# New costs for the planner of an attention, pairwise-tanh and recurrence kernel

## The chip, the cores and the metric

The kernel runs on one core of a Trainium2 chip, in fp32. The metric is the device time of one launch in microseconds (us). The core has five engines that each run their own queue of instructions in order: TensorE (PE; its weight loads are PEld), VectorE (DVE), ScalarE (ACT), GpSimd (POOL) and SyncE (SP, which issues transfers). An instruction that needs the result of another engine waits for a semaphore, and all that stands behind it in its queue waits with it.

## The reference

Eight batches of 1024 tokens of 128 channels go through two layers. Layer 0 is attention with 8 heads and two softmaxes, a feed-forward net and two layer norms. Layer 1 has an attention whose scores are sums of a tanh over all pairs of tokens, and then a recurrence over the 1024 tokens with a batch norm before it. Cut to what matters:

```python
# layer 0
scores = einsum('bhlfc,bhmgc->bhlfmg', q, k) / sqrt(c)     # 1024 x 1024 for each of 8 heads
a = softmax(softmax(scores, axis=4), axis=5)
z = einsum('bhlfmg,bhmgc->bhlfc', a, v)
z1 = layer_norm(z @ wo.T + bo + x)
x = layer_norm(relu(z1 @ w1.T + b1) @ w2.T + b2 + z1)
# layer 1, attention: t is x as tokens, B = norm(t)
Wi = einsum('bnd,ed->bne', B, W)
s = einsum('d,bijd->bij', v, tanh(Wi[:, None, :, :] + Wi[:, :, None, :]))
t = t + einsum('bij,bjd->bid', softmax(s), B)
# layer 1, recurrence: y_t = sigmoid(batch_norm(W norm(t))_t + y_{t-1} V^T), added to t
```

The pairwise tanh is the largest part: 1024 x 1024 / 2 pairs by 128 channels in each batch (the scores are symmetric, so half is computed).

## The kernel before

**Work and tiles.** `layer0(b)` walks over 8 heads and, for each head, over 8 blocks of 128 queries. A block is a chain across engines: scores on PE (L851, into one of two buffers `sc`), the first exponential on ACT (L854), sums over one axis and their reciprocal on DVE (L858, L859), the division on DVE (L862, into a pair buffer `e` in `wx`). For two blocks together follow the second exponential on ACT (L871), sums and reciprocal on DVE (L874, L875), two divisions on POOL (L885), sixteen transposes on PE (L765), four copies of banks on DVE (L777), sixteen matmuls "attend" on PE (L899) and a sum into `zs` on DVE (L906). There are 256 such pairs in all.

`layer1(b)` computes the pairwise tanh. For each block of 128 rows it builds groups of k rows: a row of `wiT` plus one column as bias, by ACT at once with the tanh (L993, one instruction a row), or added by POOL (L1000) or DVE (L996 or L1000) with one whole-group tanh on ACT behind it (L1036). The group lies in one of five slots `th`. PE then multiplies each row with `v` (L1053), four row groups side by side in a narrow tiling mode, into `sa`. When a block of rows is complete, ACT takes the exponential of `sa` (L1149), and attention, projection and statistics follow.

After the last batch there are the recurrence and the output (from L1321 on), written in plain program order.

**What sets the order.** All of this is not emitted as the loops run. Each piece is an entry in a `Plan` (class at L409): a weight in us, an engine or a choice of engines, what it reads and writes, a priority. `Plan.emit` (L455) then runs a list schedule in its own notion of time. For each entry it knows when it is ready: the planned end of what it depends on, plus `LATENCY` of the engine that made it, or `AGAIN` if that is the same engine. It takes the engine with the earliest possible start, looks at all entries there that can start within 0.15 us (`slack`) of it, and emits that with the lowest priority number; a change of mode on PE costs 0.1 in the plan (`switch`). The engine that builds the rows of a group is chosen the same way, by the earliest start. The planned times are used for nothing else: what reaches the chip is one order for each engine, and the waits that the dependencies need. Two PSUM banks `m0` and `m1` are shared by nearly all that goes through a bank (`through_bank`, L755); the plan also picks which of them is taken, by which was planned free first.

**Priorities** (`pace`, and `ROWS` and `L1` in `layer1`) are set so that layer 0 of batch b + 1 and layer 1 of batch b lie side by side over the whole middle of the run. Layer 0 of batch 0 stands alone at the start, and layer 1 of batch 7 at the end.

Of the kernel before, what the change touches and what calls it, by code (L numbers as in the profile page):

```python
# [15 lines left out]
P = 128  # L16
# [392 lines left out]
class Plan:  # L409
# [12 lines left out]

    LATENCY = {"PE": 0.28, "ACT": 0.2, "DVE": 0.15, "POOL": 0.3, "SP": 8.0}
    AGAIN = {"PE": 0.0, "ACT": 0.0, "DVE": 0.08, "POOL": 0.15, "SP": 8.0}

    def __init__(self):
        self.ops = []
# [131 lines left out]
def fast_path(ctx: ExitStack, tc: tile.TileContext, a: dict, fits):  # L561
# [222 lines left out]
    def layer0(b):  # L784
# [16 lines left out]
        for n_part, part in enumerate(parts):  # L801
# [3 lines left out]
            for h in range(H):  # L805
                L0 = pace(n_part, h)

                u, vp, kvp = us[h % 2], vps[h % 2], ("vp", h % 2)
                if alone:
                    vp, kvp = ths[3 + h // 4][:, h % 4 * N : (h % 4 + 1) * N].rearrange("p (t c) -> p t c", c=C), ("vp0", h)  # L810
                for s in range(2) if part is None else (part,):
                    cols = slice(s * 512, (s + 1) * 512)

                    def project(bank, h=h, cols=cols):
                        nc.tensor.matmul(bank, A[:, h, :], xT[:, cols], start=True, stop=True)

                    def biased(e, bank, h=h, u=u, cols=cols):
                        if e == "ACT":
                            nc.scalar.activation(u[:, cols], bank, AF.Identity, bias=ub[:, h : h + 1])
                        else:  # L820
                            nc.vector.tensor_scalar(u[:, cols], bank, ub[:, h : h + 1], None, ALU.add)

                    through_bank(project, 0.9, [kx], biased, evict(0.75), [], [("u", h % 2, s)], L0, banks)
                for s in () if alone and n_part else range(2):

                    def values(bank, h=h, s=s):
                        for i in range(4):
                            t = 4 * s + i
                            nc.tensor.matmul(
                                bank[:, i * P : (i + 1) * P], xT[:, t * P : (t + 1) * P], Wvo[:, h, :], start=True, stop=True  # L830
                            )

                    through_bank(
                        values, 0.95, [kx], copy(vp[:, 4 * s : 4 * s + 4, :]), evict(0.7), [], [kvp + (s,)], L0, banks
                    )
                for qt in qts:
                    L0 = pace(n_part, h + (qt - qts[0]) / len(qts))
                    i = (n_part * H + h) * len(qts) + qt - qts[0]
                    sc, kc = scs[i % 2], ("sc", i % 2)
                    pair, q = (b * H * NT + i) // 2 % NE, qt % 2  # L840
                    e2, st = es[pair], stat_e[pair]
                    e, ke = e2[:, q, :], ("e", pair, q)
                    k1, k2 = ke + (1,), ("e", pair, 2)
                    r1, r2 = st[:, q, 0:G], st[:, :, G : G + M]
                    sc3 = sc.rearrange("p (m g) -> p m g", g=G)
                    e3 = e.rearrange("p (m g) -> p m g", g=G)

                    def scores(_, sc=sc, u=u, qt=qt):
                        for s in range(2):
                            cols = slice(s * 512, (s + 1) * 512)  # L850
                            nc.tensor.matmul(sc[:, cols], u[:, qt * P : (qt + 1) * P], xT[:, cols], start=True, stop=True)  # L851

                    add(("PE", 1.81), scores, r=[kx, ("u", h % 2, qt // 4)], w=[kc], pri=L0)
                    add(("ACT", 1.02), lambda _, sc=sc: nc.scalar.activation(sc, sc, AF.Exp, scale=SCALE),  # L854
                        r=[kc], w=[kc], pri=L0)

                    def first_sums(_, sc=sc, r1=r1):
                        nc.vector.tensor_reduce(r1, sc.rearrange("p (m g) -> p g m", g=G), AX.X, ALU.add)  # L858
                        nc.vector.reciprocal(r1, r1)  # L859

                    def divide(_, e3=e3, sc3=sc3, r1=r1):
                        nc.vector.tensor_tensor(e3, sc3, r1.unsqueeze(1).to_broadcast([P, M, G]), ALU.mult)  # L862

                    add(("DVE", 1.6), first_sums, r=[kc], w=[k1], pri=L0)
                    add(("DVE", 1.22), divide, r=[kc, k1], w=[ke], pri=L0)
                    if q == 0:
                        continue


                    ks = [("e", pair, q) for q in range(2)]  # L870
                    add(("ACT", 1.93), lambda _, e2=e2: nc.scalar.activation(e2, e2, AF.Exp), r=ks, w=ks, pri=L0)  # L871

                    def second_sums(_, e2=e2, r2=r2):
                        nc.vector.tensor_reduce(r2, e2.rearrange("p q (m g) -> p q m g", g=G), AX.X, ALU.add)  # L874
                        nc.vector.reciprocal(r2, r2)  # L875

                    add(("DVE", 3.3), second_sums, r=ks, w=[k2], pri=L0)
                    na = next_aT()
                    aT = aTs[na]
                    for q in range(2):  # L880
                        e, ke = e2[:, q, :], ("e", pair, q)

                        def divide_again(_, e=e, r2=r2, q=q):
                            e3 = e.rearrange("p (m g) -> p m g", g=G)
                            nc.gpsimd.tensor_tensor(e3, e3, r2[:, q, :].unsqueeze(2).to_broadcast([P, M, G]), ALU.mult)  # L885

                        add(("POOL", 1.97), divide_again, r=[ke, k2], w=[ke], pri=L0)
                        for s in range(2):
                            through_bank(
                                transposes([e[:, t * P : (t + 1) * P] for t in range(4 * s, 4 * s + 4)]), 0.52, [ke],  # L890
                                copy(aT[:, 4 * s : 4 * s + 4, q * P : (q + 1) * P]), evict(0.7), [],
                                [("aT", na, q, s)], L0, banks,
                            )
                    q0 = (qt - 1) * P
                    bank = Bank(*banks)

                    def attend(part, vp=vp, aT=aT, bank=bank):
                        for t in range(4 * part, 4 * part + 4):
                            nc.tensor.matmul(bank()[:, :256], vp[:, t, :], aT[:, t, :], start=t == 0, stop=t == NT - 1)  # L899

                    def gather(_, h=h, q0=q0, bank=bank):
                        zq = zs[:, q0 : q0 + 2 * P]
                        if h == 0:
                            nc.vector.scalar_tensor_tensor(zq, bank()[:, :256], zb, xT[:, q0 : q0 + 2 * P], ALU.add, ALU.add)
                        else:
                            nc.vector.tensor_tensor(zq, bank()[:, :256], zq, ALU.add)  # L906

                    for s in range(2):
                        add(
                            ("PE", 1.81), lambda _, attend=attend, s=s: attend(s),  # L910
                            r=[kvp + (p,) for p in range(2)] + [("aT", na, q, p) for q in range(2) for p in range(2)],
                            w=[("bank", bank)], pri=L0, take=None if s else bank, wait=[kz + (qt // 4,)],
                        )
                    add(("DVE", 0.42), gather, r=[("bank", bank), kx], w=[kz + (qt // 4,)], pri=L0, give=bank)

            L0 = b - 1 - SOON
            for qh in range(2) if part is None else (part,):
                Xg, kg = X[:, 4 * qh : 4 * qh + 4, :], kX + (qh,)
                through_bank(
                    transposes([zs[:, t * P : (t + 1) * P] for t in range(4 * qh, 4 * qh + 4)]), 0.52, [kz + (qh,)],  # L920
                    copy(Xg), evict(0.7), [], [kg], L0, banks,
                )

                def affine1(Xg=Xg):
# [3 lines left out]
                layer_norm(Xg, kg, Xg, kg, qh, L0, affine1)  # L928
                z1T, k1 = zs[:, 512 * qh : 512 * qh + 512], kz + (qh,)
                through_bank(  # L930
                    transposes([Xg[:, i, :] for i in range(4)]), 0.52, [kg], copy(z1T), evict(0.7), [], [k1], L0, banks
                )
                na = next_aT()
                hT = aTs[na].rearrange("p t q -> p (t q)").rearrange("p (f q) -> p f q", q=512)
# [35 lines left out]
    def group(it, at0, r0, k, wiT, all_wi, L1, ROWS, fillers, chain, left, both, first_half):  # L970
# [27 lines left out]
        def add_rows(eng, c):  # L998
# [6 lines left out]

        each = [(c, r) for r in range(k) for c in range(4)]
        work = {
            "ACT": [(0.19 + 0.833e-3 * (w - begin[c]), lambda c=c, r=r: tanh_row(c, r)) for c, r in each],
            "POOL": [
                (0.27 + 1.62e-3 * k * (w - begin[c]), lambda c=c: add_rows(nc.gpsimd, c)) for c in range(4)  # L1010
            ],
# [37 lines left out]
        def times_v(_):  # L1049
# [12 lines left out]
        before = ["sa"] if at0 and r0 == 0 else ["sa", "sa narrow"] if at0 else ["sa"] if r0 else []  # L1062
        after = ["sa narrow"] if at0 and r0 == 0 else [] if r0 or at0 else ["sa"]
        add(
            ("PE", k * (1.67e-3 * (w - begin[0]) + 0.03 * n)), times_v, r=[("tanh", g)] + before,
            w=[("sa", it, r0)] + after, pri=L1, mode="groups", give=slot,
        )
        return ("sa", it, r0)
# [99 lines left out]
    def attention(b, it, X, kX, B, kB, E_at, L1):  # L1168

        for j0 in range(it + 1, NT, 4):  # L1170
# [1 line left out]
            through_bank(  # L1172
                transposes([E_sb[:, E_at[it] + j - it, :] for j in js]), 0.08 + 0.12 * len(js),
                [("E", it, j) for j in js],
                copy(ET[:, j0 - 1 : j0 - 1 + len(js), :]), ("DVE", 0.15 + 0.135 * len(js)), [],
                [("ET", j) for j in js], L1,
            )

# [274 lines left out]
```

## Time and profile before

| what | value |
|---|---|
| time, median of 3 runs | 5830.94 us (5828.89 to 5839.92) |
| profiled span | 5830.7 us, 96061 instructions |
| TensorE clock granted, mean | 0.97 |
| pairwise tanh on ACT, row by row (L993) | 3180 instructions, 2318.0 us |
| pairwise tanh on ACT, group by group (L1036) | 726 instructions, 1993.6 us |
| times v on PE (L1053) | 24576 matmul records, 2113.1 us |
| scores on PE (L851) | 2048 matmul records, 983.7 us |
| first sums on DVE (L858) | 512 instructions, 1213 ns each |
| transfers, all queues | 37.71 MB, mean 6 GB/s |

In the profile, a group of instructions is named by engine and line, with what it writes and reads. An idle time is put down to whoever ended it. A matmul's end is modelled, so the busy time of PE is not the time in which it could do nothing more; the distances between starts tell more. Successive ACT instructions overlap by a few tens of ns, so the sum over groups is a little over the busy time of the engine.

### The profile page before, as it was taken

What the parts mean: (1) busy time and instruction counts of PE and PEld (TensorE: products, weight loads), DVE (VectorE), ACT (ScalarE), POOL (GpSimd) and SP (SyncE); (2) the same over time, 40 slices, a digit from 0 to 9 for tenths busy, and PEclk for the clock granted to TensorE, in tenths of its full rate; (3) what the DMA queues carried; (4) which work ended last, traced back from release to release, by engine and by line L of the source; (5) the groups of instructions that cost most, each with busy time, mean ns of one, the idle gap of its engine ahead of it and who ended that gap; (6) DMA issues with size and microseconds to landing.
All of it is one profiled execution on the core that took longest, in us unless ns stands there. A gap on an engine that the chain in (4) does not pass through costs nothing.

```text
span 5830.7 us, 96061 instructions
## 1 busy us (share of the span) xinstructions
PE 5221.5 (90%) x38885; PEld 2786.1 (48%) x38885; DVE 4688.8 (80%) x6416; ACT 5291.4 (91%) x5032; POOL 3850.9 (66%) x2414
## 2 busy tenths in 40 slices
PE   9898999899989999899998999989998998987567
PEld 6555544444544455445444444545554444543125
DVE  7989766868897778868889778868798679897885
ACT  5488999999999999889999999999999998999994
POOL 2352698788867897678776887788876876671000
PEclk9999999999999999999999999999999999998999
DMA  2000000000000000000000000000000000000001
GB/s 58 1 4 1 1 1 5 3 6 1 1 5 8 1 1 1 6 6 1 1 5 5 5 1 1 5 8 1 1 1 3 6 1 1 1 21 14 1 1 63
DMA packets 27318, 37.71 MB, mean 6 GB/s; under 512 B 2464, under 2 KB 19232, under 8 KB 26864
## 3 DMA queue, kind: packets, MB, share of 16 engines
q1 hardware_dynamic: 21760, 27.99, 1.4%
q8 instruction: 307, 5.03, 0.4%
q10 hardware_dynamic: 4944, 3.16, 0.2%
q14 instruction: 147, 1.20, 0.1%
q0 software_dynamic: 160, 0.33, 0.0%
HBM read 19.41 MB, written 12.06 MB: 5 GB/s over the span
## 4 chain that ended last, share of the span: by engine, by line
PE 42%; DVE 26%; ACT 25%; issue 5%; POOL 0%; DMA 0%; DVEq 0%; ACTq 0%; POOLq 0%; SPq 0%
PE sa L1053 16%; ACT th L1036 10%; ACT th L993 10%; PE m L899 8%; PE sc L851 7%; PE m L765 4%; DVE th L996 3%; DVE th L1000 3%; DVE stat_e L874 3%; DVE aT L777 3%; DVE stat_e L858 2%; DVE wx L862 2%; ACT sc L854 2%; ACT wx L871 2%; DVE X L737 1%
## 5 line engine op out<-in xcount | busy, mean ns | idle before, releaser
L1000 POOL TENSOR_TENSOR th<-wiT 128x1024 f32<-128x1024 f32 (+58 forms) x1824 | 2795.9, 1565 | 716.0 <-PE sa L1053 674.6
L993 ACT ACTIVATE th<-wiT 128x398 f32<-128x398 f32 (+55 forms) x3180 | 2318.0, 803 | 32.2 <-PE sa L1053 29.2
L1053 PE MATMUL sa<-th,vpat 128*32 128x512 f32 (+29 forms) x24576 | 2113.1, 468 | 250.9 <-ACT th L1036 236.3
L1036 ACT ACTIVATE th<-th 128x3306 f32<-128x3306 f32 (+52 forms) x726 | 1993.6, 2768 | 113.3 <-DVE th L996 73.7
L885 POOL TENSOR_TENSOR wx<-wx,stat_e 128x1024 f32<-128x1024 f32 x512 | 996.0, 1966 | 866.9 <-DVE stat_e L875 663.5
L1053 PEld LDWEIGHTS sa<-th,vpat 128*32 128x32 f32 x24576 | 678.1, 112 | 1512.3 <-issue 834.7
L851 PE MATMUL sc<-xT,wx 128*128 128x512 f32 x2048 | 983.7, 605 | 28.3 <-DVE wx L862 27.8
L899 PE MATMUL m<-aT,wx 128*128 128x256 f32 x3584 | 873.8, 391 | 23.6 <-DVE aT L777 22.4
L899 PEld LDWEIGHTS m<-aT,wx 128*128 128x128 f32 x3584 | 663.2, 192 | 264.9 <-issue 95.3
L777 DVE COPY aT<-m 128x512 f32<-128x512 f32 x925 | 597.1, 673 | 192.6 <-PE m L765 189.9
L858 DVE TENSOR_REDUCE stat_e<-sc 128x16 f32<-128x1024 f32 x512 | 621.1, 1213 | 155.8 <-ACT sc L854 155.0
L996 DVE TENSOR_SCALAR th<-wiT 128x312 f32<-128x312 f32 (+52 forms) x1108 | 655.0, 653 | 64.2 <-PE sa L1053 63.2
L874 DVE TENSOR_REDUCE stat_e<-wx 128x128 f32<-128x2048 f32 x256 | 583.3, 2278 | 108.2 <-ACT wx L871 107.5
L765 PE MATMUL m<-ident,wx 128*128 128x128 f32 x3908 | 574.5, 283 | 89.1 <-DVE aT L777 52.8
L862 DVE TENSOR_TENSOR wx<-sc,stat_e 128x1024 f32<-128x1024 f32 x512 | 624.1, 1219 | 26.0 <-DVE stat_e L859 0.5
L765 PEld LDWEIGHTS m<-ident,wx 128*128 128x128 f32 x3908 | 435.7, 143 | 389.3 <-issue 188.6
L854 ACT ACTIVATE sc<-sc 128x1024 f32<-128x1024 f32 x512 | 513.0, 1005 | 111.5 <-PE sc L851 100.6
L871 ACT ACTIVATE wx<-wx 128x2048 f32<-128x2048 f32 x256 | 486.8, 1901 | 104.9 <-DVE wx L862 104.1
L851 PEld LDWEIGHTS sc<-xT,wx 128*128 128x128 f32 x2048 | 358.6, 193 | 361.3 <-issue 308.0
L1000 DVE TENSOR_TENSOR th<-wiT 128x1024 f32<-128x1024 f32 (+30 forms) x280 | 398.5, 1461 | 5.2 <-PE sa L1053 5.2
L733 POOL TENSOR_TENSOR stat<-stat,neg_half 128x4 f32<-128x4 f32 x64 | 66.5, 1040 | 307.0 <-DVE stat L730 287.7
L875 DVE RECIPROCAL stat_e<-stat_e 128x128 f32<-128x128 f32 x256 | 244.0, 953 | 8.8
(170 smaller groups left out, 2980.6 us busy)
## 6 DMA issues: line engine op xcount, KB each, us to landing
xT<-in_xt_dram SPq DMA_DIRECT2D x8, 512.0 KB, 3.6
th<-in_x_dram SPq DMA_DIRECT2D x8, 512.0 KB, 6.9
parked<-X SPq DMA_DIRECT2D x16, 256.0 KB, 2.0
xr<-parked SPq DMA_DIRECT2D x8, 512.0 KB, 8.2
parked_wx<-bT SPq DMA_DIRECT2D x14, 256.0 KB, 2.0
wx<-parked_wx SPq DMA_DIRECT2D x7, 512.0 KB, 3.3
out_dram<-ot ACTq DMA_DIRECT2D x8, 256.0 KB, 2.5
out_dram<-ot SPq DMA_DIRECT2D x8, 256.0 KB, 2.4
```

Source lines behind the costliest of these rows:

```text
L765: nc.tensor.transpose(bank[:, i * P : (i + 1) * P], s, ident)
L777: nc.vector.tensor_copy(dst, src)
L851: nc.tensor.matmul(sc[:, cols], u[:, qt * P : (qt + 1) * P], xT[:, cols], start=True, stop=True)
L862: nc.vector.tensor_tensor(e3, sc3, r1.unsqueeze(1).to_broadcast([P, M, G]), ALU.mult)
L874: nc.vector.tensor_reduce(r2, e2.rearrange("p q (m g) -> p q m g", g=G), AX.X, ALU.add)
L885: nc.gpsimd.tensor_tensor(e3, e3, r2[:, q, :].unsqueeze(2).to_broadcast([P, M, G]), ALU.mult)
L899: nc.tensor.matmul(bank()[:, :256], vp[:, t, :], aT[:, t, :], start=t == 0, stop=t == NT - 1)
L993: nc.scalar.activation(rows(c)[:, r, :], wiT[:, i0 + begin[c] :], AF.Tanh, bias=w_i(c, r))
L996: nc.vector.tensor_scalar(rows(c)[:, r, :], wiT[:, i0 + begin[c] :], w_i(c, r), None, ALU.add)
L1000: eng.tensor_tensor(rows(c), wiT[:, i0 + begin[c] :].unsqueeze(1).to_broadcast(shape), w_i(c).unsqueeze(2).to_broadcast(shape), ALU.add,)
L1036: lambda _: nc.scalar.activation(slot()[:, : at[4]], slot()[:, : at[4]], AF.Tanh),
L1053: nc.tensor.matmul(sa[32 * c : 32 * c + 32, s:s1], vpat[:, 31 - r0 - r : 63 - r0 - r], rows(c)[:, r, s - at0 - begin[c] : s1 - at0 - begin ...
```

## The change

Numbers only. The weights of the entries and the two tables of latencies are set anew, to durations and hand-over times as a trace of the kernel shows them. The purpose is that the planner's notion of time comes nearer to the chip's, so that its choices (what goes next, which engine adds the rows of a group, which bank is taken) are made at the right moment. No operation, buffer, priority or dependency is touched.

```diff
-    LATENCY = {"PE": 0.28, "ACT": 0.2, "DVE": 0.15, "POOL": 0.3, "SP": 8.0}
-    AGAIN = {"PE": 0.0, "ACT": 0.0, "DVE": 0.08, "POOL": 0.15, "SP": 8.0}
+    LATENCY = {"PE": 0.12, "ACT": 0.08, "DVE": 0.08, "POOL": 0.15, "SP": 8.0}
+    AGAIN = {"PE": 0.0, "ACT": 0.0, "DVE": 0.04, "POOL": 0.1, "SP": 8.0}
...
-                    add(("PE", 1.81), scores, r=[kx, ("u", h % 2, qt // 4)], w=[kc], pri=L0)
-                    add(("ACT", 1.02), lambda _, sc=sc: nc.scalar.activation(sc, sc, AF.Exp, scale=SCALE),
+                    add(("PE", 1.74), scores, r=[kx, ("u", h % 2, qt // 4)], w=[kc], pri=L0)
+                    add(("ACT", 0.98), lambda _, sc=sc: nc.scalar.activation(sc, sc, AF.Exp, scale=SCALE),
...
-                    add(("DVE", 1.6), first_sums, r=[kc], w=[k1], pri=L0)
+                    add(("DVE", 1.49), first_sums, r=[kc], w=[k1], pri=L0)
...
-                    add(("ACT", 1.93), lambda _, e2=e2: nc.scalar.activation(e2, e2, AF.Exp), r=ks, w=ks, pri=L0)
+                    add(("ACT", 1.9), lambda _, e2=e2: nc.scalar.activation(e2, e2, AF.Exp), r=ks, w=ks, pri=L0)
...
-                    add(("DVE", 3.3), second_sums, r=ks, w=[k2], pri=L0)
+                    add(("DVE", 3.25), second_sums, r=ks, w=[k2], pri=L0)
...
-                            ("PE", 1.81), lambda _, attend=attend, s=s: attend(s),
+                            ("PE", 1.74), lambda _, attend=attend, s=s: attend(s),
...
-            "ACT": [(0.19 + 0.833e-3 * (w - begin[c]), lambda c=c, r=r: tanh_row(c, r)) for c, r in each],
+            "ACT": [(0.18 + 0.833e-3 * (w - begin[c]), lambda c=c, r=r: tanh_row(c, r)) for c, r in each],
...
-            ("PE", k * (1.67e-3 * (w - begin[0]) + 0.03 * n)), times_v, r=[("tanh", g)] + before,
+            ("PE", k * (1.69e-3 * (w - begin[0]) + 0.005 * n)), times_v, r=[("tanh", g)] + before,
```

The copies of whole banks (`evict`) go from 0.7 to 0.68 at four places, and the copy of `ET` from 0.15 + 0.135 a block to 0.15 + 0.132. Untouched are, among others, the weights of the row additions on POOL and DVE, of the divisions, of the layer norms (2.3, 1.2 and 1.4 or 2.8), of the transposes (0.52) and of the projections, as well as `slack`, `switch` and all priorities.

More of the change, by code (lines that the diff above doesn't have):

```diff
@@ L833, in layer0 @@
                     through_bank(
-                        values, 0.95, [kx], copy(vp[:, 4 * s : 4 * s + 4, :]), evict(0.7), [], [kvp + (s,)], L0, banks
+                        values, 0.95, [kx], copy(vp[:, 4 * s : 4 * s + 4, :]), evict(0.68), [], [kvp + (s,)], L0, banks
                     )
@@ L890, in layer0 @@
                                 transposes([e[:, t * P : (t + 1) * P] for t in range(4 * s, 4 * s + 4)]), 0.52, [ke],
-                                copy(aT[:, 4 * s : 4 * s + 4, q * P : (q + 1) * P]), evict(0.7), [],
+                                copy(aT[:, 4 * s : 4 * s + 4, q * P : (q + 1) * P]), evict(0.68), [],
                                 [("aT", na, q, s)], L0, banks,
@@ L920, in layer0 @@
                     transposes([zs[:, t * P : (t + 1) * P] for t in range(4 * qh, 4 * qh + 4)]), 0.52, [kz + (qh,)],
-                    copy(Xg), evict(0.7), [], [kg], L0, banks,
+                    copy(Xg), evict(0.68), [], [kg], L0, banks,
                 )
@@ L930, in layer0 @@
                 through_bank(
-                    transposes([Xg[:, i, :] for i in range(4)]), 0.52, [kg], copy(z1T), evict(0.7), [], [k1], L0, banks
+                    transposes([Xg[:, i, :] for i in range(4)]), 0.52, [kg], copy(z1T), evict(0.68), [], [k1], L0, banks
                 )
@@ L1174, in attention @@
                 [("E", it, j) for j in js],
-                copy(ET[:, j0 - 1 : j0 - 1 + len(js), :]), ("DVE", 0.15 + 0.135 * len(js)), [],
+                copy(ET[:, j0 - 1 : j0 - 1 + len(js), :]), ("DVE", 0.15 + 0.132 * len(js)), [],
                 [("ET", j) for j in js], L1,
```

## The prediction

> **What bounds the kernel now.** I read the page first, then the busy time by stage, then who waited for whom inside the long stage, then the timeline for single durations.
>
> The page's busy shares (part 1):
>
> ```profile
> PE 5221.5 (90%) x38885; PEld 2786.1 (48%) x38885; DVE 4688.8 (80%) x6416; ACT 5291.4 (91%) x5032; POOL 3850.9 (66%) x2414
> ```
>
> No engine stands alone: TensorE 90%, ScalarE 91%. By stage (columns: stretch, its length, busy us and instructions of PE, PEld, DVE, ACT, POOL, then clock, DMA share, GB/s):
>
> ```profile
> 312.00:416.00 104.00, 99.55 (x513) 58.76 (x514) 88.72 (x97) 92.34 (x103) 69.91 (x40) 0.97 0.02 6
> ...
> 670.00:5236.00 4566.00, 4222.94 (x31905) 2212.93 (x31907) 3674.52 (x4812) 4327.52 (x3856) 3565.87 (x2246) 0.98 0.01 3
> 5236.00:5721.00 485.00, 317.84 (x3224) 114.51 (x3217) 387.58 (x746) 467.81 (x308) 33.05 (x20) 0.93 0.02 7
> ```
>
> Up to about 416 us batch 0's layer 0 runs with TensorE ahead of the rest. From there to 5236 us (the end of the last second exponential, L871) layer 0 of one batch and layer 1 of the one before share the engines: PE 92% and ACT 95% busy. From 5236 to 5721 ScalarE alone is full (96%). In the long stage, these are the waits (who waited for whom: us in all, times, longest), of PE, of PE's weight loads, and of ACT:
>
> ```profile
> PE sa L1053 <- ACT th L1036: 89.5, 81, 7.6
> PE m L765 <- DVE aT L777: 88.8, 59, 8.2
> ```
>
> ```profile
> PEld m L765 <- DVE aT L777: 119.2, 125, 8.5
> ```
>
> ```profile
> ACT wx L871 <- DVE wx L862: 83.4, 35, 19.2
> ACT th L1036 <- DVE th L996: 57.8, 28, 5.5
> ACT sc L854 <- PE sc L851: 44.0, 43, 6.4
> ```
>
> PE and ACT wait for each other and both for DVE, a few us at a time. So the time is the work of ACT (or PE, much the same) plus these small stalls; no single wait carries it. The timeline gives the durations that the planner's numbers stand for:
>
> ```profile
> 3005.72 1.16 PE L829 MATMUL m<-Wvo,xT 128*128 128x128 f32 x8
> ...
> 3006.91 0.69 DVE L777 COPY wx<-m 128x512 f32<-128x512 f32 x1 [0.99 <-PE m L829]
> ...
> 3009.31 1.88 PE L851 MATMUL sc<-xT,wx 128*128 128x512 f32 x4
> ...
> 3011.12 1.20 PE L1053 MATMUL sa<-th,vpat 128*32 128x464 f32 x16
> ...
> 3014.60 1.01 ACT L854 ACTIVATE sc<-sc 128x1024 f32<-128x1024 f32 x1
> ...
> 3015.66 1.21 DVE L858 TENSOR_REDUCE stat_e<-sc 128x16 f32<-128x1024 f32 x1
> ...
> 3033.94 1.88 PE L851 MATMUL sc<-xT,wx 128*128 128x512 f32 x4
> ...
> 3035.66 0.60 PE L765 MATMUL m<-ident,wx 128*128 128x128 f32 x4
> ```
>
> Scores take 3035.66 - 3033.94 = 1.72 us when a transpose follows and 3011.12 - 3009.31 = 1.81 when a times-v group follows: a change of mode costs 0.09. A hand-over PE to DVE took 3006.91 - 3006.88 = 0.03, ACT to DVE 3015.66 - 3015.61 = 0.05. The plan of before allows 0.28 and 0.2 for these, the new one 0.12 and 0.08.
>
> [...] the same four-part normalisation on DVE (L737) costs 651 ns a part on B and 1148 on ET. The change leaves those weights alone, so DVE goes on lagging its plan at these spots.
>
> **The change part by part.** No operation, buffer or dependency changes. What changes is the order on each engine and which engine adds the layer-1 rows. Counting both built programs:
>
> 1. ACT: tanh rows (L993) 3180 to 3152, whole-group tanhs (L1036) 726 to 728, tanh elements alike at 4.22 million. Eleven rows of 602 took 7.59 us in the timeline, 0.69 each, which is 0.19 + 0.833 ns an element; a group of 4096 took 3.61, that is 0.2 + the same slope. Saving: 28 x 0.19 - 2 x 0.2 = 4.9, less 0.6 for one bank copy more (594 ns): 4.3 us. Not a reason for much.
> 2. POOL row additions 1824 to 1820, DVE ones 1108 to 1116 (L996) and 280 to 284 (L1000): under 10 us more on DVE, which is 80% busy. I take it as hidden.
> 3. PE: the same matmuls; mode changes 2004 to 2038, 34 x 0.09 = 3.1 us.
> 4. DMA: one fetch of a parked batch trades places; hidden, as DMA is 1% busy in that stage.
>
> So what counts is the stalls. I cut the span at the ends of every 32nd second exponential (L871), where a batch's layer 0 ends: 416.1, 998.2, 1681.4, 2358.2, 3053.4, 3735.3, 4428.8, 5236.2 us. The lengths are 582, 683, 677, 695, 682, 694, 807. ACT's work between the same marks, summed from the order of before with the durations above (L854 1.005, L871 1.901), is 559, 667, 667, 665, 673, 685, 767. The differences are the stalls: 23, 16, 10, 30, 9, 9, 41, together 137 us. Then 416.1 + 4683 (work) + 137 + 594.5 (after 5236) = 5831, the span.
>
> The same sums over the new order:
> - First stage. PE has 401.1 us of work up to batch 0's last attend before (1.67 ns a column, a quarter of that for the times-v groups, four of which run side by side) and 394.5 after: -6.6, and PE is the fullest engine there.
> - Batches: ACT 569, 669, 671, 655, 671, 655, 792, together 4684: +1. PE has in a middle batch some 628 us and 290 changes of mode at 0.09, 654, over a clock of 0.98 667: as much as ACT, so the two cannot get ahead of each other.
> - Last stage: 148 rows, 151 groups and 504,628 elements of tanh are left before, 136, 155 and 512,220 after: -2.3 + 0.8 + 6.3 = +4.8, all on the full engine.
>
> Sum: -6.6 + 1 + 4.8 = -0.8: the work is as it was, and with the stalls of before the time would be 5830.
>
> What the order says of the stalls goes both ways. For fewer: scores come more evenly; the PE work between the scores that share a buffer (i and i+2) has its 10th and 90th percentiles at 7.3 and 33.3 us before, 9.4 and 26.0 after. The long wait of the second exponential (19.2 us at most) and of DVE behind it come from such bunching. And the new order settles into a rhythm of two batches: instruction for instruction the stretches of layer 0 of batches 3 and 5 are alike on ACT and on PE, and those of 4 and 6; before, no two were. For more: the plan leaves less slack. The PE work between the last transpose of a pair and its first attend, in which DVE must bring out the last bank, is under 1.5 us for 56 of 256 pairs before and 98 after; the shortfall to 1.5 adds to 33 us before and 59 after. A bank comes out in 0.03 + 0.69 + about 0.05 = 0.77 us if DVE is free at once, so even the tightest (0.86) hold when DVE is on time; in the trace it often is not (the 8.2 us wait).
>
> **The rivals.**
> - A, even order: the batches with 23, 30 and 41 us of stalls are the irregular ones; the median of the seven is 16. With all at the median the stalls are 7 x 16 = 112, time 5693 + 112 = 5805. If all came to the best (9): 63, 5756.
> - B, equal: order is shuffled, stalls stay near 137, time 5830. For it: the work sums to nothing, and the hand-overs that the plan now trusts are still longer than measured. Against: an order that differs in nearly every place on PE will hardly leave stalls to a few us.
> - C, tight order, slower: [...] PE now stands still at the 42 additional tight pairs; +26 us from the attends, up to 39 from the reuse of the two banks, whose shortfall to 1.5 us goes from 158 to 197. Time 5856 to 5869. For it: DVE already ends 208 us of PE waits (88.8 + 119.2). Against: those that are tight only by their plan still hold at 0.77.
>
> **How the numbers follow.** A 0.45, B 0.2, C 0.35. A leads since the old plan kept score buffers, banks and slots longer than the trace does, which may be what bunches the scores; it does not lead by much, as the slack that is given up is real, and a rhythm repeats its stalls as well as its good stretches. The forecast is A's 5805. The range goes from 5765, most of the way to every batch at the best, to 5872, just over C. Faster by over 0.2% (below 5819): A, 0.45. Within 0.2%: B, 0.2. Slower: C, 0.35.
>
> **What would show it.** Right: in the long stage the waits of L871 for L862 and of L854 for L851 shrink, ACT is over 95% busy, and the batch lengths become alike, near 680. C: the waits of PE and its loads for DVE at L765 and L899 grow beyond 208 and 75 us. The last stage should take some 599 us and the first end near 409; if either is off by 15, the step that costs the ends by their work is wrong. It is wrong altogether if ACT's row count (3152) carries the difference, or if TensorE's clock (0.97) moves.

## The result and the profile after

| | before | after |
|---|---|---|
| time, median | 5835.43 us | 6007.48 us (6006.17 to 6011.48) |
| ratio | | 1.0292, 95% interval 1.0277 to 1.0307 |
| profiled span | 5830.7 us | 6009.6 us |
| TensorE clock, mean | 0.97 | 0.96 |

The forecast was 5805 us, and the range ended at 5872. The change makes the kernel 2.9% slower. The 5835.43 us is the median of four runs, the three whose median is 5830.94 and one more.

The page of after, busy shares (part 1):

```profile
PE 5261.8 (88%) x38885; PEld 2787.4 (46%) x38885; DVE 4757.5 (79%) x6427; ACT 5287.4 (88%) x5007; POOL 3848.3 (64%) x2410
```

ACT's busy time is what it was (5291.4 before). PE's grew by 40 us for the same 38885 matmul records. Cutting the span where batch 0's and batch 7's layer 0 end (by the last second exponential, L871, as in the prediction) gives 407.9, 4989.0 and 612.7 us, against 416.1, 4820.1 and 594.6. So of 178.9 us more in the span, 168.9 lie in the long stage. Busy time by stage, after (columns as in the prediction):

```profile
408.00:5397.00 4989.00, 4511.08 (x33564) 2361.45 (x33563) 3971.38 (x5112) 4546.64 (x4252) 3668.53 (x2298) 0.96 0.01 3
5397.00:5888.00 491.00, 300.06 (x3161) 109.48 (x3164) 398.66 (x774) 463.91 (x295) 30.54 (x20) 0.93 0.02 6
```

The same stage before, with the prediction's first mark:

```profile
416.00:5236.00 4820.00, 4449.62 (x33533) 2355.73 (x33535) 3905.26 (x5124) 4544.58 (x4269) 3648.77 (x2289) 0.98 0.01 3
```

What the reader is to see: ACT works as long (4544.6, 4546.6) in a stage 169 us longer. PE is idle for 4820.0 - 4449.6 = 370 us before and 4989.0 - 4511.1 = 478 after, 108 more; and it is busy 61 us longer for nearly the same number of matmuls, at a clock of 0.96 in place of 0.98. The two together make the 169. So PE's gaps grew by 108 us, and another 61 are slower matmuls. In the long stage, who waited for whom, PE of after:

```profile
PE m L765 <- DVE aT L777: 117.5, 89, 8.3
PE sa L1053 <- ACT th L1036: 86.8, 66, 6.4
PE sc L851 <- DVE wx L862: 59.1, 43, 3.9
PE m L765 <- DVE zs L906: 36.3, 10, 8.8
PE m L899 <- DVE aT L777: 26.8, 19, 7.1
```

The same of before, where the prediction does not show them:

```profile
PE m L899 <- DVE aT L777: 21.7, 23, 3.1
PE m L765 <- DVE zs L906: 21.0, 13, 4.1
PE sc L851 <- DVE wx L862: 18.1, 17, 3.3
```

And ACT of after:

```profile
ACT th L1036 <- DVE th L996: 142.4, 40, 11.7
ACT wx L871 <- DVE wx L862: 136.4, 52, 11.5
ACT sc L854 <- PE sc L851: 51.8, 24, 7.8
```

The large waits in which DVE is late for PE or ACT are longer than before, L1036 for L996 (57.8) and L871 for L862 (83.4) most. These two are 40 and 52 waits of a few us in 5000 us. No large wait of a new kind appears. Not all have grown: PE's wait for the whole-group tanh (L1053 for L1036) went from 89.5 to 86.8 us, and some small ones fell.

The clock is a second step. The trace's clock records have two values in this stage, 1.0 and 0.5. Half clock holds for 235.5 us in 51 pieces before and for 368.6 us in 65 pieces after. With PE at half its speed in them (scores take 3.75 us in place of 1.88, below), half of the extra 133 us is lost, 67 us by this estimate, which is about the 61 us of longer busy time. One such piece of after, in stretches of 3.3 to 3.4 us:

```profile
3438.40:3441.80 3.40, 3.40 (x72) 2.76 (x70) 3.40 (x2) 3.40 (x5) 3.40 (x2) 1.00 0.01 2
3441.90:3445.30 3.40, 1.04 (x2) 0.21 (x2) 3.40 (x3) 3.40 (x4) 3.40 (x3) 1.00 0.00 0
3445.40:3448.70 3.30, 0.00 (x0) 0.00 (x0) 3.30 (x2) 3.30 (x5) 3.30 (x2) 0.50 0.00 0
3448.80:3452.10 3.30, 0.32 (x2) 0.35 (x3) 3.30 (x4) 3.30 (x2) 1.98 (x1) 0.50 0.00 0
3452.20:3455.50 3.30, 1.71 (x6) 0.82 (x5) 3.23 (x5) 1.74 (x1) 0.00 (x0) 0.50 0.00 0
3455.60:3459.00 3.40, 3.40 (x12) 0.74 (x14) 0.00 (x0) 0.00 (x0) 0.00 (x0) 0.50 0.00 0
```

And the timeline of PE there:

```profile
3441.82 1.13 PE L815 MATMUL m<-xT,A 128*128 128x512 f32 x2
3451.78 1.09 PE L765 MATMUL m<-ident,wx 128*128 128x128 f32 x4 [8.84 <-DVE zs L906]
3454.46 3.75 PE L851 MATMUL sc<-xT,wx 128*128 128x512 f32 x4 [1.59 <-DVE wx L862]
```

PE stands for 8.84 us, for a DVE sum (L906) that is queued behind five row additions; those take 10.82 us, while POOL adds rows too (8.45 us from 3442.32 on). What the sum adds was there by 3442.95, when PE's last work had ended, and it started at 3451.23. The times-v group that stands behind the transposes and the scores in PE's order had its rows, of up to 884 columns, from ACT by 3447.38 (L993), and started at 3458.14. In the second line of the stretches PE worked for 1.04 of 3.40 us, in the third the clock is at 0.50, and the scores that follow take 3.75 us in place of 1.88. So this one long gap cost PE twice.

### The profile page after: what moved, and what is told of

Its sections match the earlier page's. It is cut to its first block, busy times and chain, and to the rows that moved or that the text cites. A ratio compares the mean times of both kernels' runs of the same rounds, so it can differ in the third digit from the quotient of the medians.

```text
span 6009.6 us, 96422 instructions
## 1 busy us (share of the span) xinstructions
PE 5261.8 (88%) x38885; PEld 2787.4 (46%) x38885; DVE 4757.5 (79%) x6427; ACT 5287.4 (88%) x5007; POOL 3848.3 (64%) x2410
## 4 chain that ended last, share of the span: by engine, by line
PE 42%; DVE 31%; ACT 20%; issue 6%; POOL 1%; DMA 0%; DVEq 0%; ACTq 0%; POOLq 0%; SPq 0%
PE sa L1053 14%; ACT th L1036 9%; PE m L899 8%; PE sc L851 8%; ACT th L993 7%; PE m L765 5%; DVE th L996 4%; DVE th L1000 4%; DVE stat_e L874 3%; DVE stat_e L858 3%; DVE aT L777 3%; DVE wx L862 2%; ACT sc L854 2%; ACT wx L871 1%; DVE stat_e L875 1%
## 5 line engine op out<-in xcount | busy, mean ns | idle before, releaser
L1000 POOL TENSOR_TENSOR th<-wiT 128x1024 f32<-128x1024 f32 (+59 forms) x1820 | 2793.2, 1567 | 700.4 <-PE sa L1053 654.6
L1053 PE MATMUL sa<-th,vpat 128*32 128x512 f32 (+29 forms) x24576 | 2111.7, 470 | 268.5 <-ACT th L1036 257.2
L993 ACT ACTIVATE th<-wiT 128x128 f32<-128x128 f32 (+60 forms) x3152 | 2304.5, 804 | 42.7 <-PE sa L1053 30.7
L1036 ACT ACTIVATE th<-th 128x3048 f32<-128x3048 f32 (+36 forms) x728 | 2002.3, 2772 | 220.6 <-DVE th L996 155.1
L1053 PEld LDWEIGHTS sa<-th,vpat 128*32 128x32 f32 x24576 | 666.7, 112 | 1529.5 <-issue 871.8
L851 PE MATMUL sc<-xT,wx 128*128 128x512 f32 x2048 | 1010.6, 619 | 64.4 <-DVE wx L862 61.1
L899 PE MATMUL m<-aT,wx 128*128 128x256 f32 x3584 | 880.3, 393 | 29.1 <-DVE aT L777 26.8
L899 PEld LDWEIGHTS m<-aT,wx 128*128 128x128 f32 x3584 | 666.6, 193 | 281.3 <-issue 106.6
L996 DVE TENSOR_SCALAR th<-wiT 128x358 f32<-128x358 f32 (+51 forms) x1116 | 705.0, 694 | 78.3 <-PE sa L1053 77.6
L858 DVE TENSOR_REDUCE stat_e<-sc 128x16 f32<-128x1024 f32 x512 | 619.2, 1209 | 146.8 <-ACT sc L854 145.2
L765 PE MATMUL m<-ident,wx 128*128 128x128 f32 x3896 | 578.2, 286 | 143.6 <-DVE aT L777 68.1
L862 DVE TENSOR_TENSOR wx<-sc,stat_e 128x1024 f32<-128x1024 f32 x512 | 623.8, 1218 | 25.8 <-DVE stat_e L859 0.5
L765 PEld LDWEIGHTS m<-ident,wx 128*128 128x128 f32 x3896 | 436.6, 144 | 445.3 <-issue 197.7
L871 ACT ACTIVATE wx<-wx 128x2048 f32<-128x2048 f32 x256 | 486.8, 1901 | 147.8 <-DVE wx L862 147.2
L854 ACT ACTIVATE sc<-sc 128x1024 f32<-128x1024 f32 x512 | 512.6, 1004 | 106.0 <-PE sc L851 87.4
L851 PEld LDWEIGHTS sc<-xT,wx 128*128 128x128 f32 x2048 | 367.8, 196 | 411.0 <-issue 320.2
L1000 DVE TENSOR_TENSOR th<-wiT 128x752 f32<-128x752 f32 (+16 forms) x284 | 393.2, 1432 | 3.2 <-PE sa L1053 3.1
```

What stands on the lines that cost most here:

```text
L765: nc.tensor.transpose(bank[:, i * P : (i + 1) * P], s, ident)
L993: nc.scalar.activation(rows(c)[:, r, :], wiT[:, i0 + begin[c] :], AF.Tanh, bias=w_i(c, r))
L996: nc.vector.tensor_scalar(rows(c)[:, r, :], wiT[:, i0 + begin[c] :], w_i(c, r), None, ALU.add)
L1000: eng.tensor_tensor(rows(c), wiT[:, i0 + begin[c] :].unsqueeze(1).to_broadcast(shape), w_i(c).unsqueeze(2).to_broadcast(shape), ALU.add,)
L1036: lambda _: nc.scalar.activation(slot()[:, : at[4]], slot()[:, : at[4]], AF.Tanh),
L1053: nc.tensor.matmul(sa[32 * c : 32 * c + 32, s:s1], vpat[:, 31 - r0 - r : 63 - r0 - r], rows(c)[:, r, s - at0 - begin[c] : s1 - at0 - begin ...
```

## The experiments

All times are medians, with the ratio to runs of the kernel before on the same chip. The kernels differ only in numbers of the planner, so each has another order of all engines.

**Tables or weights, and the scatter of an order.** Theory 1: the allowances in `LATENCY` were slack that took up delays. Theory 2: the lower weights do it. Theory 3: any new order lands anywhere. The first two kernels take one half of the change each:

```diff
 # e1: before, with
-    LATENCY = {"PE": 0.28, "ACT": 0.2, "DVE": 0.15, "POOL": 0.3, "SP": 8.0}
+    LATENCY = {"PE": 0.12, "ACT": 0.08, "DVE": 0.08, "POOL": 0.15, "SP": 8.0}   # and AGAIN
 # e2: after, with both tables of before
 # e3: before, with
+    LATENCY = {"PE": 0.281, "ACT": 0.2, "DVE": 0.15, "POOL": 0.3, "SP": 8.0}
 # e4: before, with
+    def emit(self, slack=0.16, switch=0.1, stay=0.015):
```

> The kernel before with the new LATENCY and AGAIN tables, all weights as before. Theory 1 (the hand-over allowances were the slack that took up DVE's lateness): about 6000, with the ACT waits of L871 for L862 and of L1036 for L996 as large as in the changed kernel (147 and 155 us). Theory 2 (the weights, above all PE's scores and attend and DVE's first sums, do it): near 5835. Theory 3 (any new order lands anywhere within some 3%): no telling, 5800 to 6000.

> The kernel before with the new weights, LATENCY and AGAIN as before. Theory 1: near 5835. Theory 2: about 6000. Theory 3: no telling, and its difference and that of the run with the tables alone need not add to 172 us.

> The kernel before with LATENCY of PE 0.281 in place of 0.28: as a number nothing, but the order of all engines is made anew. Theories 1 and 2: within 0.5% of 5835 (5806 to 5864), as the plan is the same in its costs. Theory 3: off by 1% or more, either way.

> The kernel before with the window of choice (slack) 0.16 in place of 0.15, again a new order from the same costs. Theories 1 and 2: within 0.5% of 5835. Theory 3: off by 1% or more, either way.

| run | time | ratio, 95% interval |
|---|---|---|
| e1, new tables alone | 5959.93 | 1.0215 (1.0195 to 1.0235) |
| e2, new weights alone | 5883.85 | 1.0078 (1.0055 to 1.01) |
| e3, PE 0.281 | 5859.29 | 1.004 (1.0023 to 1.0058) |
| e4, slack 0.16 | 5827.3 | 0.9986 (0.9974 to 0.9998) |

The tables cost 126 us and the weights 50, together 176, near the 172. The two nudges move about a quarter and a third of PE's matmul records in its order (by the traces) and the time by +26 and -6. So theory 3 falls for an effect of 172 us, and I take some 30 us either way as the scatter of an order. Theory 1 holds for the larger part of the time; 50 us for the weights is a little over the scatter. Its sign did not come: in the whole of e1, ACT's waits of L871 for L862 and of L1036 for L996 are 106.9 and 92.2 us, not near 147 and 155, and the largest is that of L854 for the scores, 113.9.

**More slack than before, and which entries.**

```diff
 # before, with
+    LATENCY = {"PE": 0.42, "ACT": 0.3, "DVE": 0.225, "POOL": 0.45, "SP": 8.0}  # e5, AGAIN 0.12 and 0.225
+    LATENCY = {"PE": 0.56, "ACT": 0.4, "DVE": 0.3, "POOL": 0.6, "SP": 8.0}     # e6, AGAIN 0.16 and 0.3
+    LATENCY = {"PE": 0.28, "ACT": 0.2, "DVE": 0.08, "POOL": 0.15, "SP": 8.0}   # e7, AGAIN 0.04 and 0.1
+    LATENCY = {"PE": 0.12, "ACT": 0.08, "DVE": 0.15, "POOL": 0.3, "SP": 8.0}   # e8
```

> The kernel before with both latency tables times 1.5 (PE 0.42, ACT 0.3, DVE 0.225, POOL 0.45; again 0.12 and 0.225). Theory 1 (allowances are slack that takes up lateness): the slope of the run with the new tables alone goes on, flattening: 5760 to 5835. Rival (the tables of before are a tuned optimum, as long hand-overs hold buffers too long in the plan): 5860 or more. Scatter of a new order from the same costs, by the two nudged runs: some 25 us either way.

> The same with the tables times 2 (PE 0.56, ACT 0.4, DVE 0.3, POOL 0.6; again 0.16 and 0.3). Theory 1: no slower than 5835 by more than the scatter of 25 us, as the stalls left are few. Rival: 5900 or more, slower than with 1.5.

> The kernel before with only the DVE and POOL entries of both tables lowered as in the change (DVE 0.08, POOL 0.15, again 0.04 and 0.1). Theory 1a (slack behind DVE and POOL counts, since DVE is the one that is late): most of the 126 us of the tables, 5920 to 5960. Theory 1b (slack behind PE and ACT counts, where the entries fell by 0.16 and 0.12): near 5835.

> The kernel before with only the PE and ACT entries lowered (PE 0.12, ACT 0.08). Theory 1a: near 5835. Theory 1b: 5920 to 5960. If slack counts wherever it lies, both runs lie between, near 5890.

| run | time | ratio, 95% interval |
|---|---|---|
| e5, tables x 1.5 | 5864.47 | 1.0059 (1.0042 to 1.0076) |
| e6, tables x 2 | 5826.88 | 0.9991 (0.9981 to 1.0001) |
| e7, DVE and POOL low | 5825.96 | 0.9984 (0.9973 to 0.9996) |
| e8, PE and ACT low | 5944.58 | 1.0188 (1.0168 to 1.0208) |

Above the tables of before nothing is won: e6 lies 4 us under, e5 34 us over, at the edge of the scatter. Theory 1 had e5 at 5835 at most, its rival had e6 at 5900 or more, and neither came. Since e1 lost 126 us, the effect looks like one with a threshold. Among the tables of before it lies in the PE and ACT entries (e8: 114 of the 126 us), not in those of DVE and POOL. So my theory 1a, that slack behind DVE counts because DVE is the engine that is late, falls.

**What the PE entry has to cover.** The plan counts an entry's result as start + weight + `LATENCY`, so the arrivals have to be counted from the start of a PE entry too. Timeline of after, transposes and the copy that waits for them, and scores with their exponential (PE's lines and the waiting line):

```profile
2545.73 1.98 PE L851 MATMUL sc<-xT,wx 128*128 128x512 f32 x4
...
2547.81 1.01 ACT L854 ACTIVATE sc<-sc 128x1024 f32<-128x1024 f32 x1 [0.55 <-PE sc L851]
...
3011.32 0.63 PE L765 MATMUL m<-ident,wx 128*128 128x128 f32 x4 [0.44 <-DVE aT L777]
...
3011.99 0.69 DVE L777 COPY aT<-m 128x512 f32<-128x512 f32 x1 [0.21 <-PE m L765]
```

The copy starts 0.67 us after the first transpose, the exponential 2.08 us after the first scores matmul. Over all entries of before whose consumer waited, and with the distance to PE's next entry beside it (where that is not in the narrow mode):

| entry | PE's next entry (median) | consumer starts (5% to 90%) | old plan | new plan |
|---|---|---|---|---|
| 4 transposes (L765) | 0.49 | 0.64 to 0.71 | 0.52 + 0.28 = 0.80 | 0.52 + 0.12 = 0.64 |
| scores (L851) | 1.72 | 1.92 to 2.07 | 1.81 + 0.28 = 2.09 | 1.74 + 0.12 = 1.86 |
| attend, both halves (L899) | 3.56 | 3.65 to 3.83 | 3.62 + 0.28 = 3.90 | 3.48 + 0.12 = 3.60 |

PE is free for its next entry some 0.1 to 0.35 us before the last result can be used. The new weight 1.74 is right as the time that PE is taken, and 0.12 is generous as the gap between the end of a matmul's record and the start of its consumer (0.04 us in the median of before, on DVE and on ACT); but their sum is short of the true arrival, where the old numbers were just above it. By theory P, a consumer planned that early stands too early in its engine's queue and holds up all that is behind it, which could have run; rival A is that ACT's entry does it.

```diff
+    LATENCY = {"PE": 0.12, "ACT": 0.2, "DVE": 0.15, "POOL": 0.3, "SP": 8.0}    # e9: before with this
+    LATENCY = {"PE": 0.28, "ACT": 0.08, "DVE": 0.15, "POOL": 0.3, "SP": 8.0}   # e10: before with this
+    LATENCY = {"PE": 0.28, "ACT": 0.08, "DVE": 0.08, "POOL": 0.15, "SP": 8.0}  # e11: after with this
+    LATENCY = {"PE": 0.20, "ACT": 0.2, "DVE": 0.15, "POOL": 0.3, "SP": 8.0}    # e12: before with this
```

> The kernel before with LATENCY of PE alone lowered, 0.28 to 0.12. Theory P (the plan counts a PE entry as its weight plus this latency; in the trace transposes reach DVE 0.64 to 0.69 us after their start and scores reach ACT after 1.92 to 1.98, while the old plan has 0.80 and 2.09 for them and this one 0.64 and 1.93, so that the consumers stand too early in their queues): nearly all of the loss of PE and ACT together, 5920 to 5960. Rival A (the ACT entry does it): near 5835, within the scatter of 30 us.

> The kernel before with LATENCY of ACT alone lowered, 0.2 to 0.08. Theory P: near 5835 within 30 us, as ACT's results reach DVE and PE 0.03 to 0.05 us after its end and 0.08 still covers that. Rival A: 5920 to 5960.

> The changed kernel, all new weights and tables, with LATENCY of PE alone back at 0.28. Theory P: the loss is all but gone, 5805 to 5885 (the run with the new weights and old tables took 5884; with 0.28 scores count 2.02 in the plan and arrive after 1.92 to 1.98). Rival (the loss comes from less slack anywhere, whichever entry): 5930 or more, as ACT, DVE and POOL stay low.

> The kernel before with LATENCY of PE at 0.20, half way. Theory P: with the old weights the plan then has 0.72 for transposes, 2.01 for scores and 3.82 for the attend, all just above what the trace has (0.64 to 0.69, 1.92 to 1.98, 3.65 to 3.76), so nothing is lost: 5805 to 5865. Rival (slack counts in proportion, wherever the true value lies): half the loss, about 5890.

| run | time | ratio, 95% interval |
|---|---|---|
| e9, PE 0.12 alone | 5926.86 | 1.0155 (1.0133 to 1.0176) |
| e10, ACT 0.08 alone | 5864.85 | 1.0051 (1.0036 to 1.0067) |
| e11, after with PE 0.28 | 5933.88 | 1.0167 (1.0142 to 1.0192) |
| e12, PE 0.20 alone | 5851.33 | 1.0022 (1.0013 to 1.0031) |

PE alone costs 90 us, ACT alone no more than the scatter. Half way (e12) costs 14 us, nearer to a threshold's nothing than to half of 90, though the two lie only a scatter apart. But e11 misses: with PE back at 0.28 the changed kernel keeps some 100 us of its loss. Theory P did not allow for that; the rival, less slack anywhere, had forecast it.

**What is left.** Either it is still PE: with the lower weights, 0.28 gives 2.02 for scores and 3.76 for the attend, inside the measured spread, no longer above it (P2). Or it is the chain ACT, DVE, ACT, in which weights and tables together leave nothing (W). Or it is the luck of this order.

```diff
 # after, with
+    LATENCY = {"PE": 0.40, "ACT": 0.08, "DVE": 0.08, "POOL": 0.15, "SP": 8.0}  # f1
+    LATENCY = {"PE": 0.28, "ACT": 0.2, "DVE": 0.08, "POOL": 0.15, "SP": 8.0}   # f2
+    LATENCY = {"PE": 0.28, "ACT": 0.08, "DVE": 0.15, "POOL": 0.3, "SP": 8.0}   # f3, AGAIN 0.08 and 0.15
+    LATENCY = {"PE": 0.121, "ACT": 0.08, "DVE": 0.08, "POOL": 0.15, "SP": 8.0} # f4
```

> The changed kernel with LATENCY of PE at 0.40, all else as changed. The new PE weights are 0.07 lower for an entry of scores and 0.14 for an attend; with 0.40 the plan has 2.14 for scores and 3.88 for the attend, as the old one had 2.09 and 3.90. Theory P2 (what is left of the loss at PE 0.28, some 90 us, is also PE's results being planned too early): 5830 to 5875. Theory W (it is the chain ACT, DVE, ACT, where the new weights and entries together have 3.89 us from the first exponential to the second, against 4.27 before): stays at 5900 to 5950.

> The changed kernel with PE 0.28 and ACT 0.2 in LATENCY, DVE and POOL as changed. Theory W: some slack is back in the chain (4.01 us in place of 3.89, before 4.27), so about half of the 90 us goes: 5870 to 5910. Theory P2: no change from the run with PE 0.28 alone, 5934 within 30.

> The changed kernel with PE, DVE and POOL as before (0.28, 0.15, 0.3; again 0.08 and 0.15), ACT alone low at 0.08. Theory W: as with ACT restored, about half of the 90 us goes: 5870 to 5910 (the chain has 4.00). Theory P2: 5934 within 30.

> The changed kernel with LATENCY of PE 0.121 in place of 0.12: the same costs, another order. Theories P2 and W: the loss belongs to the costs, 5960 to 6030. Rival (some of the 172 us is the luck of one order): 5900 to 5950, the sum of what PE alone took and the scatter.

| run | time | ratio, 95% interval |
|---|---|---|
| f1, after with PE 0.40 | 5826.06 | 0.9985 (0.9977 to 0.9993) |
| f2, after with PE 0.28, ACT 0.2 | 5903.83 | 1.0113 (1.0083 to 1.0144) |
| f3, after with PE 0.28, DVE and POOL as before | 5884.59 | 1.0077 (1.0053 to 1.0102) |
| f4, after with PE 0.121 | 5964.18 | 1.0212 (1.0181 to 1.0243) |

f1 settles the larger question: one number, PE's entry, takes the changed kernel from 6007 to 5826 us, with all new weights and all other low entries in place. Theory W had 5900 to 5950 for it. Busy time of f1 in its long stage:

```profile
407.00:5240.00 4833.00, 4458.29 (x33586) 2343.27 (x33584) 3967.09 (x5151) 4561.14 (x4322) 3640.05 (x2255) 0.98 0.01 3
```

PE's idle time is 4833.0 - 4458.3 = 375 us, as before (370), and the clock is back at 0.98, with 222 us at half. ACT's waits in f1:

```profile
ACT th L1036 <- DVE th L996: 89.7, 37, 6.9
ACT wx L871 <- DVE wx L862: 57.1, 25, 6.8
ACT sc L854 <- PE sc L851: 35.3, 27, 4.4
```

The waits for DVE fell from 142 and 136 us to 90 and 57, though no number of DVE was changed back. So "DVE is late" was what the page showed, and it could be ended without a change to DVE's numbers. DVE's time beside a busy POOL does not tell the kernels apart either: DVE operations on L737, L996, L1000 and L1155 during which POOL was busy take together some 830 us before, 890 after and 890 in f1.

f2 and f3 give back 30 and 49 us. That is what W had forecast and not P2 (f3 is outside its 30 us, f2 at its edge), so slack elsewhere stands in for part of it where PE's is short; where PE's is ample (f1) its lack costs nothing. Whether ample slack at DVE or ACT alone would make up for a PE entry of 0.12 was not run. f4 shows that 43 of the 172 us may be this order's luck, and that the larger part belongs to the costs.

**Scores or attend.** The last two put one PE weight back each, beside PE 0.28:

```diff
-                            ("PE", 1.74), lambda _, attend=attend, s=s: attend(s),
+                            ("PE", 1.81), lambda _, attend=attend, s=s: attend(s),   # g1
-                    add(("PE", 1.74), scores, r=[kx, ("u", h % 2, qt // 4)], w=[kc], pri=L0)
+                    add(("PE", 1.81), scores, r=[kx, ("u", h % 2, qt // 4)], w=[kc], pri=L0)  # g2
```

> The changed kernel with LATENCY of PE 0.28 and the weight of each half of an attend back at 1.81, so that the plan has 3.90 for an attend (as before) and 2.02 for scores. If the attend's 3.76 was the entry that came too early in the run with PE 0.28 alone (the trace has 3.65 to 3.83): near 5840, within 30. If the scores' 2.02 was it (the trace has 1.92 to 2.08): near 5934. If margin counts wherever it lies: between, near 5885.

> The changed kernel with LATENCY of PE 0.28 and the weight of scores back at 1.81: the plan has 2.09 for scores, as before, and 3.76 for an attend. If the scores' 2.02 came too early: near 5840, within 30. If the attend's 3.76 did: near 5934. If margin counts wherever it lies: near 5885.

g1 took 5951.33 us (1.0205, 1.0181 to 1.0229), g2 5878.43 (1.008, 1.0057 to 1.0104). Giving the attend its weight back wins nothing; the scores give back 56 of the 100 us, so g2 lies 7 us from the forecast of "margin wherever it lies" and 38 from that of the scores alone, while g1 fits the scores and not the margin. All kernels sorted by when the plan has the scores arrive at ACT (weight plus PE's entry; the trace has 1.92 to 2.08):

| planned arrival | PE's entry alone changed, or none | other entries or weights low too | tables all higher |
|---|---|---|---|
| 1.86 | | 6007 (after), 5964 (f4) | |
| 1.93 | 5927 (e9) | 5945 (e8), 5960 (e1) | |
| 2.01, 2.02 | 5851 (e12) | 5884 (e2), 5885 (f3), 5904 (f2), 5934 (e11), 5951 (g1) | |
| 2.09 | 5830 (before), 5827 (e4), 5859 (e3) | 5826 (e7), 5865 (e10), 5878 (g2) | |
| 2.14 and more | | 5826 (f1) | 5864 (e5), 5827 (e6) |

Below the measured arrival the time climbs, in the first column by 14 us down to 2.01 and by 90 down to 1.93 (each against before in its own set). Above it, all lie within some 35 us of before except g2, at 49. In one row the other entries still move the time by up to 100 us (2.01 and 2.02), so the planned arrival of the scores is not the only thing that counts.

What stays open is which of PE's results it is. PE's entry in `LATENCY` moves scores, transposes, attends and the times-v groups (L1053) together; transposes and times-v were not tried alone. The times-v groups, whose weight the change lowers too, have the same gap: in before a waiting POOL row addition (L1000) starts 0.21 us (median) after PE's next entry, and the plan takes a slot `th` as free from that result on.

How a consumer planned 0.1 us too early turns into waits of several us is open as well. If scores were what comes late, ACT should wait longer for them. In the long stage it does not: L854 waited 44.0 us for L851 before, 51.8 after and, with PE's entry alone lowered (e9):

```profile
ACT sc L854 <- PE sc L851: 16.7, 13, 4.0
```

The copies of transposes on DVE do wait more often and longer in after than before:

```profile
DVE aT L777 <- PE m L765: 179.1, 171, 3.4
DVE aT L777 <- PE m L765: 258.9, 245, 5.4
```

In f1 they are back at 183.6 us, but e9, which loses 90 us, has only 186.0. So it is shown that PE's entry alone can cost 90 us (e9) and that raising it alone undoes the whole loss (f1); that a consumer which stands too early holds up what is behind it is seen in single cases only (the times-v group above, ready by 3447.38 and started at 3458.14), and that this is what costs the 90 us is my estimate: these direct waits do not show it.

No version is clearly better than before: f1 (0.9985), e7 (0.9984) and e4 (0.9986) all lie 4 to 7 us under it, less than the scatter of an order.

## Why the prediction was wrong

- **The work** was right. Row counts, mode changes and the ends came as worked out: first end 407.9 us (409 expected), last stage 612.7 (599, off by 14), ACT's busy time the same. None of it carries the difference.
- **The rhythm of two batches** was right and did not help. The batches with alike orders take 719 and 716, and 707 and 707 us, not near 680; a settled order repeats its stalls. The stalls over ACT's work, by the prediction's sum, are 27, 22, 48, 52, 45, 52 and 60 us, some 305 together, where I had 137 before and took 112.
- **The sum of ACT's work** was too large by 138 us for the kernel before: 4683 against 4544.6 busy. Most of that comes from adding up times of records (1.005 us for the first exponential, 1.901 for the second, 3.61 for a group of 4096), but back to back the next ACT instruction starts 96 ns (median, long stage of before) ahead of the end of a record, and not a few tens. ACT's idle time was 4820.0 - 4544.6 = 275 us before, twice my 137, and 442 after. The growth is 167 us by either count, so this is not what went wrong.
- **The step that failed** is the hand-over of PE's results: "PE to DVE took 3006.91 - 3006.88 = 0.03", from which rival B had "the hand-overs that the plan now trusts are still longer than measured", and A that the old plan "kept score buffers, banks and slots longer than the trace does". I measured from the end of the last matmul's record. The plan counts from the start of the entry plus a weight that is PE's occupancy, which ends some 0.2 us sooner. By that measure the new plan is short by 0 to 0.07 us for transposes, by 0.06 to 0.21 for scores and by 0.05 to 0.23 for the attend, and the old plan was just long enough for all three. I had both numbers in my own fence: the scores' record of 1.88 us and the 1.72 us to the next entry. What the runs showed in its place: lowering PE's entry alone costs 90 us (e9), and raising it alone takes the changed kernel from 6007 to 5826 us (f1). Which of PE's results it is, and by which waits it costs so much, stays open.
- **Even order, fewer stalls (A)**: the scores did come more evenly (10th to 90th percentile 9.4 to 26.0 us of PE work), but it did not shorten the time: f1 and e9 are about as even, and they differ by 101 us. Evenness says nothing here. A's signs failed: ACT's waits of L871 for L862 and of L854 for L851 grew (83.4 to 136.4 us, 44.0 to 51.8) instead of shrinking, and ACT was busy for 91% of the long stage and not over 95%.
- **Tight order (C)** had the right side, but 26 to 39 us of the 172. Its sign came true: the waits of PE and its loads for DVE at L765 and L899 grew, but only from 208 to 223 us and from 75 to 94. The lines of PE's loads in after:

```profile
PEld m L765 <- DVE aT L777: 105.4, 89, 9.1
PEld m L899 <- DVE aT L777: 66.7, 81, 7.5
```

  Giving the attend its weight back (g1) won nothing. The 26 and 39 us that I took from the shortfall left ACT's own waits for DVE out, which grew by 85 and 53 us (L1036 for L996, L871 for L862), and the clock.
- **The clock** was put at nothing: the prediction divides by 0.98 and says that it is wrong if TensorE's clock moves. It moved from 0.98 to 0.96 in the long stage, and PE's work there took 61 us longer, of the 169.
- **The range** reached to C and stopped there, as if C's sum were a bound. A new order costs some scatter by itself (26, 6 and 43 us in the three nudges), and the one number I could not bound was the slack. Neither was in it.

## What to carry to other kernels

When a planner's costs are taken from a trace, an entry has two numbers: how long it holds its engine, and when its result reaches the next one. On PE they differ by some 0.2 us here, and shortening one without lengthening the other plans consumers before their data are there. Take the upper end of the measured arrivals for the sum of the two: tables twice as long cost nothing here, and a PE entry shorter by 0.16 us cost 90 us. Where the other costs are cut too, that end was not enough (g2), and more was (f1). Before explaining a new order, nudge a number that means nothing, to know how far an order moves the time by itself, and do not take the engine that the waits name for the cause before a run has shown it.

## What the runs showed of the hardware that I had not expected

- In these two runs half clock came without one long gap of PE, too. The pieces of half clock in the long stage of after lasted 3.41 us (36 of 65) or two, three or four times that (19, 6 and 4). In the 3.41 us ahead of each of the 65, as long as the shortest piece, PE was idle for 56% (10th percentile) to 93% (90th), 71% in the median (71% in before's 51 too); only 15 had a PE gap there that had lasted over 3.4 us, and in one the longest gap had lasted 1.2 us. Ahead of the other 50 stood shorter gaps, which a count of the long ones leaves out.
- Some DVE operations took four to five times as long while POOL worked, others no longer at all: a part of the normalisation (L737) 0.34 us alone and 1.31 while POOL was busy during some of it, the product on L1155 0.28 and 1.35; the first sums (L858) 1.21 either way (after, means).
